# Four sparse attention layers on one core: the first layer's late part in pairs of blocks, list numbers on ScalarE, constants ahead of the statistics

## The chip, the cores and the metric

The kernel runs on one core of a Trainium2 chip. The metric is the device time of one execution in microseconds. Before the change it is 2178.64 us, the median of three runs (2177.56 to 2183.43). The core's engines, as they are called here: PE multiplies matrices, DVE (VectorE) does elementwise work, maxima and sums along the free axis, ACT (ScalarE) does functions, copies and casts, POOL (GpSimd) here issues the gathers and scatters through memory, and SP issues the plain transfers. Each engine works through its own instructions in order and waits on semaphores of the others.

## The reference, cut to what matters

Four graph layers run over the same 4096 nodes of 256 features; each adds to `x` what it computes from the normed `x` and the adjacency. About 277 blocks-of-128 neighbour slots cover all edges, since the adjacency is sparse (a node has itself and a handful of others).

```python
h = jnp.maximum(_layernorm(x, axis=-1), 0.0)
x = x + _L0_gnn_ref(h, adj, L0_gnn_W, L0_gnn_a)      # 4 heads
...
def _L0_gnn_ref(h, adj, W, a):
    Wh = (h @ W).reshape(n, heads, d)
    e = s_i[:, None, :] + s_j[None, :, :]
    e = jax.nn.leaky_relu(e, negative_slope=0.2)
    e = jnp.where((adj == 0)[:, :, None], -jnp.inf, e)
    alpha = jax.nn.softmax(e, axis=1)
    out = jnp.einsum('ijh,jhd->ihd', alpha, Wh).reshape(n, heads * d)
    return jax.nn.elu(out)
```

Layers 1 to 3 are of the same kind, with other scores and weights.

## The kernel before, in words

**Scan** (`lists`, `scan`). The adjacency, 64 MB of int32, is read row block by row block (32 blocks of 128 nodes). ACT casts it to 8 bits (`cast`), PE turns each 512 columns into position codes in PSUM, with the constants `mark`, `places` and `stands` (`marks`), DVE takes the eight greatest of every 256 columns (L485) and `merge` (L493, L495) the best 24 of a row. `number(r)` (L502, L505) turns these codes into node numbers, clamped to 0..n; it is two POOL instructions. The order on ACT, PE and DVE is written out by hand as a list of steps: `plan(engine, at, ...)` puts a piece of work at step `at`, four steps to half a row block, eight to a block, 256 in all for the scan's own work, and `run` issues it. POOL's instructions are ordered by the program's scheduler, except that gathers keep their written order (`in_turn`).

**First layer, early part** (`table`, `early`). While the scan goes on, the first layer's table (normed rows times `W`, with the score sums) is made and written to memory, and for each pair of blocks POOL gathers the first six neighbours (`EARLY`, 12 gathers a pair), which DVE, ACT and PE weigh and add up.

**Placing** (`sort`, `to_place`). Nodes are sorted by their number of neighbours. POOL scatters each row block to its sorted place, one scatter to a block: from step 236 on the first 12, the rest after the scan. Two spans of four steps (240 to 243 and 256 to 259) are left free of scatters. When all have landed, `reload` (L693, L707) reads the lists and rows back, in the order `FIRST`.

**First layer, late part** (`layer(0)`). After the sort a block `b` needs `CAPS[b]` slots, so `CAPS[b] - 6` late ones: 17, 8, 7, 6, 6, 5, 5, 4, 4, 4, five times 3, four times 2, four times 1, and none for blocks 23 to 31; 93 in all. POOL issues one gather to a slot (L757), up to four blocks ahead (`AHEAD`), into a ring of slots. A block then passes through

- `scores`: score sums, leaky relu, maximum, difference (DVE L916, L925, L927, L947, L948), exponential (ACT L955);
- `weigh`: sum, reciprocal, shares (DVE L992 to L998), the block's own part (L1023), shares times gathered rows (L1037), and the sum over slots on PE (L1028, L1047);
- `settle`: elu (ACT L1061, L1062, DVE L1072, L1073), norm (DVE L571, L572, L578, L581 to L587, ACT L577, L579), relu (ACT L734), transposes (PE L742), copy (ACT L744);
- `advance`: product with layer 1's weights (PE L750), then the sum into `x` (DVE L1089), two small copies (ACT L1090, L1091), and one scatter of the row into layer 1's table (POOL, L767).

The stages of several blocks are interleaved by hand; the scatter of a block stands in POOL's queue between the gathers of later blocks. Blocks without a late slot (K = 0) pass with L981, L983 in place of scores and weigh.

**Layers 1 to 3** do the same with all 277 slots each. Layer 1's first gather waits until the last row of its table has landed.

Of the kernel before, what the change touches and what calls it, by code (L numbers as in the profile page):

```python
# [19 lines left out]
P = 128  # L20
# [32 lines left out]
FIRST = [31, 30, 29, 28, 0] + [b for k in range(1, 14) for b in (28 - k, k)] + [14]  # L53
# [18 lines left out]
class Sparse:  # L72
# [30 lines left out]
    def constants(self):  # L103
        nc, const = self.nc, self.const
        self.ident = const.tile([P, P], F32, name="s_ident")
        make_identity(nc, self.ident)
        self.ident_bf = const.tile([P, P], BF16, name="s_ident_bf")
        nc.vector.tensor_copy(self.ident_bf, self.ident)
        self.mark = const.tile([P, P], BF16, name="s_mark")
        nc.vector.tensor_scalar(self.mark, self.ident, MARK, None, ALU.mult)  # L110

        self.below = const.tile([P, P], BF16, name="s_below")
        ones = self.ones = const.tile([P, P], BF16, name="s_ones")
        nc.vector.memset(ones, 1.0)
        nc.vector.memset(self.below, -1.0)
        nc.gpsimd.affine_select(
            out=self.below, in_=self.below, pattern=[[-1, P]], compare_op=ALU.is_ge, fill=0.0,
            base=0, channel_multiplier=1,
        )
        self.eps = const.tile([P, 1], F32, name="s_eps")  # L120
        nc.vector.memset(self.eps, EPS)

# [116 lines left out]
    def scan(self, w0, a0):  # L239
# [32 lines left out]
        nc.vector.memset(self.eps, EPS)  # L272
        xl = lambda g: self.keep[:, 4 * g : 4 * (g + 1), 0:D]
# [22 lines left out]
        for k in range(4):  # L296
            stats(0, k)
        next(norms[0])
        scaled(0)
        *_, (self.we0, _) = first  # L300
        cast(2)
        self.constants()
        for g in range(1, 3):
            for k in range(4):
                stats(g, k)
            next(norms[g])
            scaled(g)
            cast(2 * g + 2)
        later = self.weights()
# [47 lines left out]
        for r in range(nt):  # L357
            plan("pool", 8 * (r + 1), lambda r=r: self.number(r))
        whole, last = [], 0
        for j in range(nt // 2):  # L360
            begin = max(4 * (10 + j), 4 * (4 * j + 4))
            stages = self.early(j)
            step = lambda stages=stages: next(stages)
            plan("pool", begin, step)

            last = max(last + 13 if j else begin + 24, begin + 17)
            plan("dve", last, step)
            for k in range(3):
                plan("dve", last + 2 + k, step)
            for k in range(EARLY + 1):  # L370
                plan("pe", last + 6 + 2 * k, step)
            plan("act", last + 2 * EARLY + 8, step)
            whole.append(last + 2 * EARLY + 8)
# [6 lines left out]
        for at in range(end + 1):  # L380
# [30 lines left out]
            if t > halves - 6 and t not in (halves - 4, halves):  # L411
# [85 lines left out]
    def number(self, r):  # L497

        nc, n = self.nc, self.n
        ids = self.pool.tile([P, TOPK - 1], F32, name=f"s_ids_{r}", tag="ids")  # L500
        self.in_turn(
            nc.gpsimd.tensor_scalar(ids, self.top[:, r, 1:], MARK, MARK + n, ALU.max, ALU.min)  # L502
        )
        self.in_turn(
            nc.gpsimd.tensor_scalar(  # L505
                self.ids[:, r, 0 : TOPK - 1], ids, -1.0, MARK + n, ALU.mult, ALU.add
            )
# [57 lines left out]
    def norms_of(self, pool, x, m, name):  # L565

        nc = self.nc
        mv = pool.tile([P, m, 2], F32, name=f"s_mv_{name}", tag="mv", bufs=2)
# [7 lines left out]
        y = pool.tile([P, 3, m], F32, name=f"s_y_{name}", tag="y", bufs=2)  # L576
# [6 lines left out]
        rn = pool.tile([P, 2 * m], F32, name=f"s_rn_{name}", tag="rn", bufs=2)  # L583
# [103 lines left out]
    def reload(self):  # L687

        nc, tc, nt, n = self.nc, self.tc, self.nt, self.n
        by_place = self.placed.rearrange("(b p) k -> p b k", p=P)  # L690
        near = self.near = self.big.tile([P, nt, 32], U32, name="s_near")
        for a, b in ((0, 2), (nt - 2, nt), (2, nt - 2)):
# [13 lines left out]
            for k in {0: [], nt - 2: FIRST[:5], 2: FIRST[5:]}[a]:  # L706
# [70 lines left out]
    def layers(self):  # L777
        tc, nc, nt = self.tc, self.nc, self.nt
        with ExitStack() as ctx:
            big = self.big = ctx.enter_context(tc.tile_pool(name="s_big", bufs=1))  # L780
            self.pool = ctx.enter_context(tc.tile_pool(name="s_main", bufs=2))
# [7 lines left out]
            rx = big.tile([P, nt, D + WL], F32, name="s_rx")  # L789
# [9 lines left out]
            with tc.manual_schedule():  # L799
                self.reload()  # L800
                for l in range(4):
# [3 lines left out]
    def slots(self, l, b):  # L805
        return max(CAPS[b] - EARLY, 0) if l == 0 else CAPS[b]

    def layer(self, l):
# [6 lines left out]
        order = ORDER if l else FIRST  # L815
        todo, held, at = list(order), {}, 0
        made = []

        def fill(i):
            nonlocal at  # L820
            while todo and nt - len(todo) <= i + AHEAD:
# [13 lines left out]
                k0 = EARLY if l == 0 else 0  # L835
                for k in range(K):
                    at_k = self.near[:, j, k0 + k : k0 + k + 1]
# [33 lines left out]
        for i in range(nt):  # L871
            fill(i)
            b, c, d, e = (order[k] if k >= 0 else None for k in (i, i - S, i - N, i - N - 1))
# [13 lines left out]
        z, y, x, w = order[-1:-5:-1]  # L887
# [14 lines left out]
    def scores(self, l, b, mine, g):  # L902


# [3 lines left out]
        if K == 0:  # L908
            return None
        e = pool.tile([P, TOPK, H], F32, name=f"s_e_{l}_{b}", tag="e", bufs=3)  # L910
        ek = e[:, : K + 1, :].rearrange("p k h -> p (k h)")
        if l < 3:
            src = mine[:, D + H : D + 2 * H]
            if l > 0:
                nc.vector.tensor_tensor(e[:, K, :], mine[:, D : D + H], src, ALU.add)
# [8 lines left out]
            el = ek if l > 0 else ek[:, : K * H]  # L924
            nc.vector.scalar_tensor_tensor(el, el, slope, el, ALU.mult, ALU.max)  # L925
            if l == 0:
                nc.vector.tensor_copy(e[:, K, :], mine[:, D : D + H])  # L927
# [45 lines left out]
    def weigh(self, l, b, me, g, p):  # L973
# [5 lines left out]
        if K == 0:  # L979

            nc.vector.reciprocal(tot, self.before[b])  # L981
            mev = pool.tile([P, D], F32, name=f"s_me_{l}_{b}", tag="me", bufs=4)
            nc.vector.tensor_tensor(  # L983
                mev.rearrange("p (h d) -> p h d", h=H), me.rearrange("p (h d) -> p h d", h=H),
                tot.unsqueeze(2).to_broadcast([P, H, D // H]), ALU.mult,
            )
            return mev
        else:
            by_head = p[:, : K + 1, :].rearrange("p k h -> p h k")
            if l == 0:  # L990
                was = pool.tile([P, H], F32, name=f"s_was_{b}", tag="was", bufs=2)
                nc.vector.tensor_tensor(was, p[:, K, :], self.before[b], ALU.mult)  # L992
                nc.vector.tensor_reduce(tot, by_head[:, :, :K], AX.X, ALU.add)
                nc.vector.tensor_tensor(tot, tot, was, ALU.add)
            else:
                nc.vector.tensor_reduce(tot, by_head, AX.X, ALU.add)  # L996
            nc.vector.reciprocal(tot, tot)  # L997
            nc.vector.tensor_tensor(  # L998
                by_head, by_head, tot.unsqueeze(2).to_broadcast([P, H, K + 1]), ALU.mult
            )  # L1000
            mine = p[:, K, :]
# [13 lines left out]
        pairs = l > 1  # L1015
        full = pairs and K % 2 == 0
        if pairs and not full:
            mev = g[:, K, v0 : v0 + D]
        else:
            mev = pool.tile([P, D], F32, name=f"s_me_{l}_{b}", tag="me", bufs=4)  # L1020
        if full:
            nc.vector.tensor_scalar(mine, mine, 0.5, None, ALU.mult)  # L1022
# [4 lines left out]
        if not pairs:  # L1027
            nc.tensor.matmul(acc, lhsT=self.ident, rhs=mev, start=True, stop=(K == 0))  # L1028
        elif full:
# [4 lines left out]
        for k0 in range(0, K, AT_ONCE):  # L1034
# [5 lines left out]
            for k in range(k0, k0 + m, 2 if pairs else 1):  # L1040
                if pairs:
                    nc.tensor.matmul(  # L1042
                        both, lhsT=self.ident, rhs=g[:, k : k + 2, v0 : v0 + D],
                        start=(k == 0 and not full), stop=(k + 2 >= K),
                    )
                else:
                    nc.tensor.matmul(  # L1047
                        acc, lhsT=self.ident, rhs=g[:, k, v0 : v0 + D],
                        start=False, stop=(k + 1 == K),
                    )  # L1050
        return both if pairs else acc

    def settle(self, l, b, acc, made):
# [4 lines left out]
        if l == 0:  # L1058

            ex = pool.tile([P, D], F32, name=f"s_ex_{b}", tag="ex", bufs=2)  # L1060
            nc.scalar.activation(ex, acc, AF.Exp)  # L1061
            nc.scalar.activation(ex, ex, AF.Copy, bias=-1.0)  # L1062
# [8 lines left out]
        if l == 0:  # L1071
            nc.vector.scalar_tensor_tensor(ex, ex, 0.0, xt, ALU.min, ALU.add)  # L1072
            nc.vector.scalar_tensor_tensor(xt, acc, 0.0, ex, ALU.max, ALU.add)  # L1073
        else:
            for part in (acc[:, 0, :], acc[:, 1, :]) if l == 2 else (acc,):
                nc.vector.tensor_tensor(xt, xt, part, ALU.add)
        into = self.rows[b][:, 0:D] if l == 0 else None
        yield from self.normed(pool, xt, f"{l + 1}_{b}", into=into)

    def advance(self, l, b, ht, made):  # L1080
# [5 lines left out]
        if l == 1:  # L1086
            ps = self.times(ht, self.we1, W, name)
            yield
            nc.vector.tensor_tensor(xt, xt, ps[:, 0:D], ALU.add)  # L1089
            nc.scalar.copy(mine[:, D:W], ps[:, D:W])  # L1090
            nc.scalar.copy(self.listed[b][:, W:], self.near[:, b, 0:TOPK])  # L1091
            made.append((self.tab[1], self.own(b), self.listed[b]))
        elif l == 2:
# [591 lines left out]
```

## Time and profile before

| what | value |
|---|---|
| median of three runs | 2178.64 us |
| the profiled execution | 1824.07 us |
| its span, first to last instruction | 1822.3 us |
| POOL, indirect transfers | 924 late gathers and those of layers 1 to 3 (953 ns each), 192 early gathers (946 ns), 96 scatters |
| DVE busy | 1379.5 us, 76% |
| POOL busy | 1185.3 us, 65% |
| PE busy | 991.5 us, 54% |
| ACT busy | 424.5 us, 23% |

The profiled execution is 354.6 us shorter than the median of the runs. Nothing in the profile says where this difference lies; all durations below are from the profiled execution.

The stages, read from the first and last starts of the lines: scan with early part from 0 to 417 us, placing until 429.7, late part of the first layer from 431.7 (first late gather) to 644.3 (first gather of layer 1), then layers 1 to 3.

To read it: a row of the timeline gives start, duration, engine, line, operation, what it writes and reads with its shape, and in brackets the idle time of the engine before it and what ended it. A row of the waits gives the engine and line that waited, what for, the time in total, how often, and the longest. A row of the windows gives, for a stretch, each engine's busy time and number of instructions.

### The profile page before, as it was taken

The page shows a single profiled execution, that of the slowest core. Times are in us where ns is not written, and L with a number is a line of the kernel's source. Part 1 is how long each engine was busy: PE and PEld are TensorE (multiplying, and loading weights), DVE is VectorE, ACT ScalarE, POOL GpSimd, SP SyncE. Part 2 cuts the span into 40 slices and gives each one's busy share as a digit, 9 for nine tenths or more (in the row PEclk, how much of TensorE's full clock was granted, in tenths as well). Part 3 has the DMA queues.
Part 4 walks back from the last instruction along what each step waited for, and adds up shares of the span by engine and source line. Part 5 has one row for each costly group of instructions (what it writes and reads, how often), then busy time and mean ns, then how long its engine had stood idle before and what let it go on. Part 6 is the DMA issues. An engine that isn't in the chain of part 4 may idle for free. (4 is left out here: it accounts for less than half of the span.)

```text
span 1822.3 us, 14325 instructions
## 1 busy us (share of the span) xinstructions
PE 991.5 (54%) x2551; PEld 476.5 (26%) x2551; DVE 1379.5 (76%) x3900; ACT 424.5 (23%) x1240; POOL 1185.3 (65%) x1324
## 2 busy tenths in 40 slices
PE   4877777752676602222323067888684344565455
PEld 3523333220454401111111023434342111221122
DVE  6889989952689718888888167887885587887777
ACT  5864434101244401111111012222222000000000
POOL 1067756676666267777775577777772577776774
PEclk9989889875788855555555578899897676777777
DMA  9899877347633144444444344444443576666763
GB/s 327 280 394 350 288 272 254 101 141 238 190 97 95 45 104 125 131 130 132 131 131 111 76 118 132 130 137 131 137 128 109 159 217 208 208 208 182 210 205 108
DMA packets 123018, 312.89 MB, mean 172 GB/s; under 512 B 31237, under 2 KB 49672, under 8 KB 122921
## 3 DMA queue, kind: packets, MB, share of 16 engines
q0 software_dynamic: 68064, 207.46, 40.2%
q1 hardware_dynamic: 54856, 104.44, 16.3%
q14 instruction: 74, 0.60, 0.1%
q8 instruction: 24, 0.39, 0.1%
HBM read 276.80 MB, written 35.00 MB: 171 GB/s over the span
## 5 line engine op out<-in xcount | busy, mean ns | idle before, releaser
L757 POOL DMA_INDIRECT s_ring<-s_tab,s_near x924 | 883.9, 957 | 352.8 <-issue 192.0
L1042 PE MATMUL s_acc<-s_ring,s_ident 128*128 128x512 f32 x588 | 319.6, 698 | 184.9 <-issue 96.2
L1042 PEld LDWEIGHTS s_acc<-s_ring,s_ident 128*128 128x128 f32 x588 | 130.6, 228 | 369.6 <-issue 244.8
L757 POOL DMA_INDIRECT s_g<-s_tab,s_keep x192 | 183.2, 954 | 65.0 <-issue 56.5
L485 DVE MAX8 s_cand<-s_pt 128x8 f32<-128x256 f32 x512 | 181.6, 414 | 17.5 <-PE s_pt L483 17.0
L1037 DVE TENSOR_TENSOR s_ring<-s_ring,s_shares 128x2048 f32<-128x2048 f32 (+7 forms) x121 | 187.4, 1572 | 0.0
L742 PE MATMUL s_pht<-s_ident,s_h 128*128 128x128 f32 x128 | 34.3, 361 | 247.9 <-ACT s_h L734 247.9
L750 PE MATMUL s_ps<-s_we_l,s_ht 128*128 128x264 f32 x256 | 115.6, 596 | 92.5 <-ACT s_ht L744 92.5
L1008 DVE SCALAR_TENSOR_TENSOR s_acc<-s_ring,s_p,s_acc 128x256 f32<-128x256 f32 x277 | 135.7, 490 | 9.7
L263 ACT ACTIVATE s_low<-s_raw 128x1024 fp8e4<-128x1024 int32 x128 | 134.2, 1049 | 20.6 <-DMA s_raw<-in_adj_dram 17.3
L558 PE MATMUL s_ae<-s_g,s_ident 128*128 128x512 f32 x192 | 116.1, 701 | 37.3 <-DVE s_g L549 37.3
L478 PE MATMUL s_pt<-s_low,s_mark 128*128 128x512 fp8e4 x256 | 108.1, 422 | 33.8 <-DVE s_cand L485 13.3
L916 DVE TENSOR_TENSOR s_e<-s_ring,s_rx 128x8 f32<-128x8 f32 (+12 forms) x87 | 15.7, 181 | 140.1 <-DMA s_ring<-s_tab,s_near 135.3
L935 DVE TENSOR_TENSOR s_ring<-s_ring,s_shares 128x2048 f32<-128x2048 f32 (+7 forms) x48 | 81.1, 1690 | 48.1 <-DMA s_ring<-s_tab,s_near 32.4
L750 PE MATMUL s_ps_kv<-s_wkv,s_ht 128*128 128x512 f32 x128 | 79.2, 750 | 69.9 <-ACT s_ht L744 69.9
L483 PE MATMUL s_pt<-s_places,s_stands 128*128 128x512 bf16 x256 | 106.6, 416 | 1.4 <-DVE s_stands L455 1.4
L955 ACT ACTIVATE s_shares<-s_e 128x32 f32<-128x32 f32 (+8 forms) x87 | 17.5, 201 | 353.3 <-DVE s_e L948 353.3
L577 ACT ACTIVATE s_y<-s_mv,s_eps 128x1 f32<-128x1 f32 x96 | 28.3, 294 | 294.6 <-DVE s_mv L572 294.6
L750 PEld LDWEIGHTS s_ps<-s_we_l,s_ht 128*128 128x128 f32 x256 | 64.3, 277 | 123.9 <-ACT s_ht L744 113.7
L742 PEld LDWEIGHTS s_pht<-s_ident,s_h 128*128 128x128 f32 x128 | 18.3, 172 | 287.8 <-ACT s_h L734 271.8
L938 DVE TENSOR_REDUCE s_e<-s_ring 128x32 f32<-128x2048 f32 (+7 forms) x48 | 81.2, 1692 | 1.7
L502 POOL TENSOR_SCALAR s_ids<-s_top 128x23 f32<-128x23 f32 x32 | 10.1, 314 | 108.7 <-DVE s_top L493 108.4
(195 smaller groups left out, 1692.2 us busy)
## 6 DMA issues: line engine op xcount, KB each, us to landing
s_raw<-in_adj_dram SPq DMA_DIRECT2D x128, 512.0 KB, 8.1
s_ring<-s_tab,s_near POOLq DMA_INDIRECT x924, 3.0
s_rx<-s_placed SPq DMA_DIRECT2D x32, 262.0 KB, 6.8
s_tab<-s_kv SPq DMA_DIRECT2D x32, 256.0 KB, 2.6
s_tab<-s_keep SPq DMA_DIRECT2D x8, 528.0 KB, 6.9
s_tab<-s_rx SPq DMA_DIRECT2D x32, 132.0 KB, 2.0
s_keep<-in_x_dram SPq DMA_DIRECT2D x8, 512.0 KB, 4.1
s_vself<-s_tab SPq DMA_DIRECT2D x32, 128.0 KB, 2.6
```

Source lines behind the costliest of these rows:

```text
L263: nc.scalar.activation(low[r][:, ts(h, n // 4)], raw.pop(q), AF.Copy, saturate=False, accum_out=self.sums[:, r, h : h + 1],)
L478: nc.tensor.matmul(pt, lhsT=self.mark, rhs=lo[:, ts(g, IB)], start=True, stop=False)
L483: nc.tensor.matmul(pt, lhsT=self.stands[:, g, :], rhs=self.places, start=False, stop=True)
L485: nc.vector.max(out=cand[:, g * (IB // CH) + k, :], in_=pt[:, ts(k, CH)])
L558: nc.tensor.matmul(acc, lhsT=self.ident, rhs=g[:, :, k, 0:D], start=False, stop=(k == E - 1))
L750: self.nc.tensor.matmul(ps[:, :width], lhsT=ht[:, c, :], rhs=w[:, c, :], start=(c == 0), stop=(c == KC - 1),)
L757: return self.nc.gpsimd.indirect_dma_start(out=out, out_offset=None, in_=table[:, :], in_offset=bass.IndirectOffsetOnAxis(ap=idx, axis=0),)
L935: nc.vector.tensor_tensor(kq, kq, q.unsqueeze(1).to_broadcast([P, m, D]), ALU.mult)
L938: nc.vector.tensor_reduce(e[:, k0 : k0 + m, :], kq.rearrange("p k (h d) -> p k h d", h=4), AX.X, ALU.add)
L1008: nc.vector.scalar_tensor_tensor(acc, g[:, k, 0:D], p[:, k, :], acc, ALU.mult, ALU.add)
L1037: nc.vector.tensor_tensor(v, v, p[:, k0 : k0 + m, :].unsqueeze(3).to_broadcast([P, m, H, D // H]), ALU.mult)
L1042: nc.tensor.matmul(both, lhsT=self.ident, rhs=g[:, k : k + 2, v0 : v0 + D], start=(k == 0 and not full), stop=(k + 2 >= K),)
```

## The change

Three things change.

**The late part** becomes a function of its own, `late`, that runs over entries of one or two blocks. Two blocks share an entry only if they have the same number of late slots. An entry of two runs `scores`, the shares, the own part, the elu and the second half of the norm as one instruction over both blocks; the products of shares and rows, the statistics, the relu, the transposes, the product with the weights and the sum into `x` stay one to a block. PE sums slot `k` of both blocks in one matmul of 512 columns. Gathers are issued two entries ahead, and the stages of an entry follow each other within three entries. The order of the blocks changes with it.

**The list numbers** (`number`) move from POOL to ACT, as two relus, two steps later; the early gathers of pair `j` come three steps later; the scatters of placing skip only steps 256 to 259.

**Constants first.** `constants()` is called ahead of the first group's statistics; the first group's weight sums come after its `cast`.

Names of small tiles get the group's size, and the branches for the first layer leave `layer`, `scores`, `weigh`, `settle` and `advance`.

```diff
-FIRST = [31, 30, 29, 28, 0] + [b for k in range(1, 14) for b in (28 - k, k)] + [14]
+LATE = [
+    (30, 31), (28, 29), (0,), (26, 27), (1,), (24, 25), (2,), (3, 4), (23,), (5, 6), (7, 8),
+    (9,), (10, 11), (12, 13), (14,), (15, 16), (17, 18), (19, 20), (21, 22),
+]
...
-        for k in range(4):
-            stats(0, k)
-        next(norms[0])
-        scaled(0)
-        *_, (self.we0, _) = first
-        cast(2)
         self.constants()
-        for g in range(1, 3):
+        for g in range(3):
             for k in range(4):
                 stats(g, k)
             next(norms[g])
             scaled(g)
             cast(2 * g + 2)
+            if g == 0:
+                *_, (self.we0, _) = first
...
-            plan("pool", 8 * (r + 1), lambda r=r: self.number(r))
+            plan("act", 8 * (r + 1) + 2, lambda r=r: self.number(r))
...
-            begin = max(4 * (10 + j), 4 * (4 * j + 4))
+            begin = max(4 * (10 + j), 16 * (j + 1) + 3)
...
-            if t > halves - 6 and t not in (halves - 4, halves):
+            if t > halves - 6 and not nt // 2 * 16 <= at < nt // 2 * 16 + 4:
...
-        self.in_turn(
-            nc.gpsimd.tensor_scalar(ids, self.top[:, r, 1:], MARK, MARK + n, ALU.max, ALU.min)
-        )
-        self.in_turn(
-            nc.gpsimd.tensor_scalar(
-                self.ids[:, r, 0 : TOPK - 1], ids, -1.0, MARK + n, ALU.mult, ALU.add
-            )
+        nc.scalar.activation(a, self.top[:, r, 1:], AF.Relu, bias=self.over)
+        nc.scalar.activation(
+            self.ids[:, r, 0 : TOPK - 1], a, AF.Relu, bias=self.none, scale=-1.0
         )
...
+    def late(self):
...
+        def fill(i):
+            while todo and todo[0] <= i + 2:
...
+        def scores(i):
...
+            nc.vector.tensor_tensor(
+                near, gathered(i)[:, :, :, D : D + H],
+                src.unsqueeze(2).to_broadcast([P, m, K, H]), ALU.add,
+            )
+            nc.vector.scalar_tensor_tensor(near, near, 0.2, near, ALU.mult, ALU.max)
+            nc.vector.tensor_copy(e[:, :, K, :], most)
...
+        def weigh(i):
...
+            for u in range(m):
+                for k0 in range(0, K, AT_ONCE):
...
+            for k in range(K):
+                nc.tensor.matmul(
+                    acc, lhsT=self.ident, rhs=g[:, :, k, 0:D], start=False, stop=(k + 1 == K)
+                )
...
+        def settle(i):
+            nc.scalar.activation(ex, acc, AF.Exp)
+            nc.scalar.activation(ex, ex, AF.Copy, bias=-1.0)
+            yield
+            nc.vector.scalar_tensor_tensor(ex, ex, 0.0, xt, ALU.min, ALU.add)
+            nc.vector.scalar_tensor_tensor(xt, acc, 0.0, ex, ALU.max, ALU.add)
...
+            yield
...
+            ps = [self.times(ht[:, u], self.we1, W, f"1_{i}_{u}") for u in range(m)]
+            yield
+            first = LATE[i][0]
+            for u in range(m):
+                nc.vector.tensor_tensor(xt[:, u, :], xt[:, u, :], ps[u][:, 0:D], ALU.add)
...
+            for b in LATE[i]:
+                self.send(self.tab[1], self.own(b), self.listed[b])
+            yield
...
+        for i in range(len(LATE) + 3):
+            fill(i)
+            go_on(i - 2)
+            if i < len(LATE):
+                scores(i)
+            go_on(i - 1)
+            go_on(i - 3)
+            go_on(i - 2)
+            if i < len(LATE):
+                weigh(i)
+                del held[i]
+            go_on(i - 1)
```

`go_on(i)` runs entry `i`'s `settle` to its next `yield`: the first stage is the exponential on ACT, the second elu and statistics, the third relu and transposes, the fourth the copy and the product, the fifth the sum into `x` and the scatters.

## The prediction

> **What bounds the kernel now.** The chain of waits on the page covers only 1% of the span, so it can't be followed back. I read the windows by stage first, to see which engine is full where; then the waits of DVE and POOL in the stages that change; then the timeline at the seams.
>
> ```profile
> core 0: us, PE busy (x) PEld busy (x) DVE busy (x) ACT busy (x) POOL busy (x), PEclk, DMA share, GB/s
> 60.00:80.00 20.00, 19.31 (x97) 13.81 (x96) 17.38 (x65) 19.12 (x45) 0.52 (x2) 1.00 0.91 284
> ...
> 340.00:385.00 45.00, 33.57 (x90) 12.04 (x87) 42.53 (x111) 1.47 (x4) 30.61 (x36) 0.80 0.39 128
> 385.00:431.00 46.00, 17.57 (x27) 6.54 (x26) 9.68 (x21) 1.32 (x3) 32.31 (x37) 0.65 0.46 165
> ```
>
> The scan is DVE's (42.5 of 45 us), but for a stretch from 60 us in which ACT and PE are full. From 385 to 431 DVE is nearly idle: POOL's queue of gathers and scatters sets the end of the placing.
>
> ```profile
> 383.79 0.96 POOL L647 DMA_INDIRECT s_placed<-s_keep,s_pos  x1 [0.30 <-issue]
> 384.78 0.34 POOL L502 TENSOR_SCALAR s_ids<-s_top 128x23 f32<-128x23 f32 x1
> ...
> 386.50 1.08 POOL L757 DMA_INDIRECT s_g<-s_tab,s_keep  x1 [0.49 <-issue]
> ```
>
> The last list is sorted on DVE at 381.06 (end of L493), yet its gathers start at 386.50: POOL is still at six scatters, then at four number instructions. The 12 gathers and 20 scatters behind run without a gap to 427.3.
>
> In the late part (431.7 to 644.3) DVE is busy 146.6 of the 181 us from 463.5 on, and some 15 more are the 0.03 us between its instructions. POOL has 93 gathers at 1.257 us (0.953 and a gap of 0.30) and 32 scatters at about 1.29: 158 us. So both are near the bound; POOL's wait list tells who leads:
>
> ```profile
> POOL s_tab L767 <- ACT s_rx L1091: 36.7, 14, 5.6
> ```
>
> The scatters wait, mostly at the end, for blocks that come out of DVE's chain. One block with K=4 on DVE:
>
> ```profile
> 548.71 0.17 DVE L916 TENSOR_TENSOR s_e<-s_ring,s_rx 128x16 f32<-128x16 f32 x1
> ...
> 549.53 0.41 DVE L1089 TENSOR_TENSOR s_rx<-s_rx,s_ps 128x256 f32<-128x256 f32 x1
> 549.86 0.44 DVE L1072 SCALAR_TENSOR_TENSOR s_ex<-s_ex,s_rx 128x256 f32<-128x256 f32 x1
> ...
> 551.55 0.15 DVE L992 TENSOR_TENSOR s_was<-s_shares,s_rx 128x4 f32<-128x4 f32 x1
> 551.62 0.16 DVE L993 TENSOR_REDUCE s_t<-s_shares 128x4 f32<-128x16 f32 x1
> 551.82 0.16 DVE L994 TENSOR_TENSOR s_t<-s_t,s_was 128x4 f32<-128x4 f32 x1
> 552.01 0.18 DVE L997 RECIPROCAL s_t<-s_t 128x4 f32<-128x4 f32 x1
> ...
> 553.91 0.15 DVE L581 TENSOR_TENSOR s_y<-s_y 128x1 f32<-128x1 f32 x1
> ...
> 554.57 0.16 DVE L916 TENSOR_TENSOR s_e<-s_ring,s_rx 128x4 f32<-128x4 f32 x1
> ```
>
> From start to start that is 5.86 us, and only 1.13 of it is the gathered rows (L1037, 0.27 a slot): a block costs about 4.75 us however few slots it has.
>
> **The late part on DVE.** The 5.86 us divide by starts into scores 0.82, L1089 0.33, elu 0.94, statistics 0.68, L578 0.07, L992 to L998 0.89, L1023 0.34, L1037 1.13, L581 to L587 0.66. A pair does scores, L578, shares and the norm's end once instead of twice: 2.44, less 0.2 for the wider rows (L916 to L948 go from 0.16 at 128x8 to 0.21 at 128x28). The elu's two instructions and L1023 go from two of 256 columns (0.42) to one of 512; the nearest row is L541, 0.68 at 128x512: 0.45 saved. Statistics back to back are 0.56 instead of 0.68 (from the scan's 4.87 to 5.96): 0.12. Together 2.8 us for each of nine pairs with slots, 25. Pairs without slots save 1.5; two of the four lie behind block 0's gathers, so 3. Sum: 28 us of DVE work.
>
> Here a rule stands against the row. The Trainium skill (Perfetto Trace Analysis, Optimizing Scalar/DVE Operations) prices an instruction's overhead on DVE at about 60 ns on SBUF. A pair drops 18 instructions, so the rule gives an estimate of 1.1 us for a pair, 10 for nine. The trace has both: L992 to L993, which don't need each other, start 0.07 apart; L993 to L994 to L997, each needing the last, 0.20. The dropped instructions are mostly such chains, so I take the rows. The 4-dimensional operands are not unknown: the early part's L526 to L549 are of this form over two blocks (0.21 to 0.27 for the small ones).
>
> **The late part on POOL.** The work is unchanged, 158 us, but its order is not. The head is as before: block 0's 17 gathers share the DMA with the 32 row loads (share 1.03), and DVE gets them at 463.5 (it waits 12.2 us there today). By then POOL has sent entries 0 to 4, 25 gathers, and the next in its queue is entry 0's two scatters. They need L1089 of entry 0, which on DVE now stands behind scores and weigh of block 0 (1.0, wait for the shares 0.7, 1.3, and 4.8 for 17 slots), the elu of entry 1 (2.8) and the norm's end and L1089 (1.4): 475.5, with ACT's copies 476. So POOL idles some 12 us; before, it had 33 gathers out by its first scatter at 474.06. From 476 the last gather is 68 gathers and the 21 scatters ahead of it away: 68 x 1.257 + 21 x 1.29 = 112.6, 588.6. I went through the entries with these prices: from entry 2 to 13 POOL leads (12 gathers and two scatters are 17.7 us for a pair of K=6, DVE needs 10.3), DVE from entry 13, whose gathers land at about 562.5 (3.1 us after issue). In a turn of the loop DVE does scores and weigh of one entry, the elu of the one before, the norm's end of the second before and L1089 of the third; by the pieces above, seven turns from there cost 7.9, 7.1, 7.0, 8.1, 7.2, 7.5 and 4.2 us to the elu of the last entry: 611.5. The last two entries then go through relu (two of 0.5), transposes, copy 0.58, four products of 0.5 and L1089 one after the other, about 9 us, and two scatters with landing 4.8: layer 1 starts at 625. Before: 644.3. **Late part: 19 us less.** PE is not in the way: a pair's slot is one matmul of 0.59 (L558, 128x512) for two of 0.38.
>
> Cover: a pair's shares (ACT L955) have only L1089 on DVE beside them (0.33 or 0.66), where elu and statistics (1.7) hid them; a single entry may show 0.3, six times 2 us at most, and in POOL's stretch nothing.
>
> **Numbers on ACT.** Two ACT instructions for a list: nearest L577, with a pointer bias, 0.30; they replace 0.30 and 0.23 on POOL. At step 8r+10 ACT would wait for the sort of step 8r+7; in 36 to 82 us ACT reaches that step just after the sort (Ln at 40.36, sort done 39.8; 58.50 against 57.9). Its casts are 8 to 28 steps ahead, and its exponentials wait for DVE anyway, so what queues behind it is not hurt. But from 60 to 82 ACT idles only 1.35 of 22 us: two lists add 0.9, so I put **+1 us** (bounds 0 and 3).
>
> **Placing.** With the free span 240 to 243 gone, all 12 early scatters go out from 351.2 on, 15.4 us, ending at 366.6; the 12 gathers of pair 14 (3 steps later, behind them) to 381.6; DVE meets them at 381 and waits 3 us, which nothing needs. The last list is ready at 381.06 + 0.6 on ACT; the last gathers run 382 to 397 instead of 386.5 to 401.5, the 20 scatters to 422.6. **-4.6 us** (bounds -6 and 0, if the scheduler puts scatters between). The three steps of delay cost nothing: POOL starts when the list is there.
>
> **Constants first.** Ten DVE instructions, 2.4 us, move from 12 to 14.4 into the idle time before 4.87, pushing the first statistics by some 0.6. The next statistics wait for `x` at 15.35 and the first relu comes at 24.15 behind `x` of group 2, so the gain is hidden: 0. The transfers keep their order. The two memsets lie there too. Fewer buffers for the own part in layers 2 and 3 (4 to 3), and the new tile pool behind `late`, fall into layer 1's wait of 37.5 us or wait for nothing: 0.
>
> **Sum:** 1824.07 - 19 - 4.6 + 1 = 1801.5, so -22.6. The runs stand 354.6 above the profiled execution, and no view shows where; I carry it as it is: 2178.64 - 22.6 = **2156 us**. If it stretched everything alike (factor 1.194), it would be 2152.
>
> **Rivals.**
> - *DVE's 28 us all arrive* (POOL's head stall is filled): late part -30, 2178.6 - 33.6 = 2145. For it: POOL idled some 22 us before, too. Against: two scatters stand in front of 68 gathers.
> - *POOL takes the late part's gain*: only the placing's remains, 2175. For it: POOL's 158 us against 181.
> - *Slower*: POOL's queue, two entries deep instead of four blocks, stops at every scatter of entries 3 to 13, as the 14 waits on ACT L1091 did, 2.6 us each: 11 x 2.6 = 29, so +6, 2185. It decides above 2 us an entry. For it: each scatter now waits for two L1089 and three ACT copies behind the exponential of the next sum. Against: in my pass DVE is 5 to 10 us ahead there.
> - *The numbers stall ACT* so that casts come late: each of 32 waits would need to cost 0.7 us of DVE time to take the gain; 13.3 us of PE's waits on DVE say DVE leads.
>
> **Chances.** Forecast (2144 to 2167) 0.62; more (below) 0.10; the gain mostly lost 0.14, of which some 0.08 lies within 0.3% (6.5 us, what a measurement can tell); slower by more 0.14. So faster 0.78, same 0.08, slower 0.14. The range takes in the scaled sum and the lost gain and leaves the slower case out: 2134 to 2174.
>
> **What would show it.** Right: the gap between the late part's first gather and layer 1's first falls from 212.6 to some 193; a POOL gap of about 12 us near 464 to 476; DVE's pair at 7 to 8 us; the last early gather some 4.6 us earlier relative to the last sort; 60 to 85 us 1 us longer. Wrong: POOL gaps before scatters in the middle, DVE waits on L955 above 0.5, or waits on L750 in every entry.

## The result, and the profile after

| | changed | before | ratio, 95% interval |
|---|---|---|---|
| median, 12 runs each | 2186.31 us (2174.53 to 2193.06) | 2180.94 us (2176.24 to 2187.58) | 1.0027 (1.0008 to 1.0046) |
| forecast | 2156.0 us (2134 to 2174) | 2178.64 us | 0.990 |

The gain of 22.6 us did not come; the change costs some 5 us, about 0.3%.

**The chips on which this was measured showed two kinds of execution:** the unchanged kernel took 1824.4 to 1825.1 us (medians) on three of them and 2149.6 and 2171.1 us on two, and no execution lay between. The profile of before that the prediction was read from (1824.07 us) is like the first kind, the runs beside it and the result above like the second. Below they are "the 1825 kind" and "the 2150 kind", and a ratio is always between kernels on one chip. Stages are read from one profiled execution of each run.

The page of the changed kernel was taken on the 2150 kind (span 2187.5 us). Its windows, in the columns of before (length, then busy time and instructions of PE, PEld, DVE, ACT, POOL; granted clock, DMA share, GB/s), for the stretch with ACT and PE full, for the whole late part and for layer 1:

```profile
60.00:80.00 20.00, 19.89 (x96) 15.05 (x97) 16.99 (x63) 19.70 (x47) 0.00 (x0) 0.91 0.92 278
...
490.00:719.00 229.00, 116.13 (x352) 73.35 (x352) 129.17 (x422) 62.31 (x192) 122.13 (x125) 0.74 0.40 115
719.00:1223.00 504.00, 90.12 (x192) 46.86 (x192) 286.80 (x984) 53.45 (x192) 262.64 (x277) 0.50 0.33 90
```

And the late part and layer 1 of the first profile of before, in the same view:

```profile
431.00:644.00 213.00, 126.58 (x424) 90.70 (x424) 153.90 (x620) 78.34 (x279) 122.08 (x125) 0.76 0.43 124
644.00:1015.00 371.00, 90.13 (x192) 46.83 (x192) 287.52 (x984) 53.40 (x192) 264.13 (x278) 0.50 0.46 122
```

Layer 1 has the same instructions in both, and the same busy times to 1.5 us on every engine, yet it takes 504 us instead of 371. The granted clock is 0.50 in both. So the 133 us are idle time, not slower work. In the late part the edit did to DVE what it was meant to: 198 instructions fewer and 24.7 us less busy. But the stretch is 229 us instead of 213. (The clock of 0.91 in the first row doesn't belong to the kind: the same kernel has 1.00 there in e4, on the 2150 kind, and 0.91 in e9, on the 1825 kind.)

What POOL waits for in that stretch (total us, times, longest):

```profile
POOL s_tab L772 <- ACT s_rx L959: 34.5, 6, 16.0
POOL s_ring L762 <- issue: 24.1, 78, 0.6
POOL s_tab L772 <- DMA s_tab<-s_rx,s_near: 19.5, 11, 1.8
POOL s_tab L772 <- issue: 12.9, 12, 2.6
```

The third line is a scatter (L772) that waits for another scatter's landing. The profile of before has that once in its late part, for 1.1 us:

```profile
POOL s_tab L767 <- DMA s_tab<-s_rx,s_near: 1.1, 1, 1.1
```

### The profile page after: what moved, and what is told of

Read it like the earlier page. It is cut to its first block, busy times and chain, and to the rows that moved or that the text cites. A ratio compares the mean times of both kernels' runs of the same rounds, so it can differ in the third digit from the quotient of the medians.

```text
span 2187.5 us, 13885 instructions
## 1 busy us (share of the span) xinstructions
PE 1001.9 (46%) x2462; PEld 464.9 (21%) x2479; DVE 1359.4 (62%) x3704; ACT 425.2 (19%) x1217; POOL 1163.0 (53%) x1260
## 4 chain that ended last, share of the span: by engine, by line
DVE 23%; issue 10%; another core or an unknown queue 7%; PE 7%; POOL 5%; DMA 2%; ACT 1%; DVEq 0%; POOLq 0%; SPq 0%; ACTq 0%
POOL s_ring L762 5%; DVE s_acc L1160 4%; PE s_acc L1189 4%; DVE s_ring L1185 3%; DVE s_ring L1103 2%; PE s_ps_kv L755 2%; DVE s_e L1106 2%; DMA s_ring<-s_tab,s_near 1%; DVE s_rx L1209 1%; DVE s_st L575 1%; PE s_ps_q L755 1%; DVE s_kv L1228 1%; DVE s_m L1115 1%; DVE s_y L586 1%
## 5 line engine op out<-in xcount | busy, mean ns | idle before, releaser
L1185 DVE TENSOR_TENSOR s_ring<-s_ring,s_shares 128x2048 f32<-128x2048 f32 (+7 forms) x96 | 159.1, 1685 | 0.0
L1103 DVE TENSOR_TENSOR s_ring<-s_ring,s_shares 128x2048 f32<-128x2048 f32 (+7 forms) x48 | 81.1, 1690 | 51.1 <-DMA s_ring<-s_tab,s_near 32.1
L755 PEld LDWEIGHTS s_ps<-s_we_l,s_ht 128*128 128x128 f32 x256 | 68.9, 292 | 185.7 <-ACT s_ht L749 77.6
L491 PE MATMUL s_pt<-s_places,s_stands 128*128 128x512 bf16 x239 | 102.0, 427 | 0.0
L581 ACT ACTIVATE s_y<-s_mv,s_eps 128x1 f32<-128x1 f32 (+1 forms) x83 | 24.5, 295 | 387.7 <-DVE s_mv L576 306.2
L1178 PE MATMUL s_acc<-s_me,s_ident 128*128 128x512 f32 x60 | 42.1, 791 | 100.9 <-issue 35.4
L1123 ACT ACTIVATE s_shares<-s_e 128x40 f32<-128x40 f32 (+7 forms) x64 | 13.2, 206 | 323.3 <-DVE s_e L1116 143.0
L772 POOL DMA_INDIRECT s_tab<-s_rx,s_near x32 | 31.7, 990 | 74.9 <-ACT s_rx L959 34.5
```

The source lines that it names most:

```text
L491: nc.tensor.matmul(pt, lhsT=self.stands[:, g, :], rhs=self.places, start=False, stop=True)
L755: self.nc.tensor.matmul(ps[:, :width], lhsT=ht[:, c, :], rhs=w[:, c, :], start=(c == 0), stop=(c == KC - 1),)
L1103: nc.vector.tensor_tensor(kq, kq, q.unsqueeze(1).to_broadcast([P, m, D]), ALU.mult)
L1185: nc.vector.tensor_tensor(v, v, p[:, k0 : k0 + m, :].unsqueeze(3).to_broadcast([P, m, H, D // H]), ALU.mult)
```

## The experiments

Theory A at the outset: the profile of before is not typical, and the idle time swallows what the edits save. Theory B: POOL's shallower queue stops at its scatters. Theory C: the late part gains as forecast and the scan loses it. Theory D came after the first four runs: in a pair, the second scatter waits for the first one to land.

**The two kernels again (e1, e4), and each half of the change alone (e2, e3).** All on one chip of the 2150 kind. e2 takes `late`, `LATE` and what goes with them and leaves the scan as before; e3 the reverse.

```
e2:  plan("pool", 8 * (r + 1), lambda r=r: self.number(r))      as before; late() of the change
e3:  plan("act", 8 * (r + 1) + 2, lambda r=r: self.number(r))   and constants() first; layer(0) as before
```

> The kernel before, unchanged, profiled once more. Theory A: the execution of 1824 us, from which every duration of the prediction came, is not what this kernel usually does; this profile comes out near 2180 us, with idle time on DVE, PE and ACT that no wait explains from about 100 us on, as in the profile of the changed kernel, and with layers 1 to 3 at about 1460 us (1467 in the changed kernel) instead of 1178. Rival B: the profile of before is typical and the change alone brings the idle time; this one comes out near 1824 us again.

> The late part in pairs, with the numbers on POOL, the old steps of gathers and scatters, and the constants behind the first statistics as before. Theory A (both parts are swallowed by idle time of all engines): within 0.3% of before. Theory B (POOL's queue of two entries stops at the scatters): slower than before by 5 to 15 us, the late part itself longer than in before. Theory C (the late part gains as predicted, the scan loses it): faster by some 15 to 20 us.

> The scan of the change (numbers on ACT, early gathers three steps later, free span moved, constants first) with the late part of before. Theory A: within 0.3% of before. Theory B: faster by up to 5 us. Theory C (ACT's wait for the sort holds the casts or the exponentials up): slower by 20 to 25 us.

> The changed kernel, unchanged, profiled on the same chip as the three others, for its stages. Theory A: layers 1 to 3 take within 1% of what they take in before's second profile, late part and scan differ by a few us each. Theory B: late part longer than before's by 10 us or more. Theory C: late part shorter by 15 us or more, the time to the first late gather longer by 20 or more.

Measured: e1 2153.56 us and e4 2148.79 us (one execution each), e2 ratio 1.0002 (0.9976 to 1.0028), e3 ratio 1.0051 (1.0021 to 1.0081). C falls: the late part gains nothing there (228.6 us in e2, 221.9 in e1), and the scan's part alone loses. e1, the kernel before, is itself at 2153 us, so the change did not bring the idle time. The timeline of DVE in e1, merging one list, shows how it looks:

```profile
115.22 0.28 DVE L495 MATCH_REPLACE8 s_cand<-s_top,s_cand 128x128 f32<-128x128 f32 x1
116.82 0.29 DVE L493 MAX8 s_top<-s_cand 128x8 f32<-128x128 f32 x1 [1.32 <-DVE s_cand L495]
118.22 0.09 DVE L495 MATCH_VALUE_LOAD s_cand<-s_top,s_cand 128x8 f32 x1 [1.11 <-DVE s_top L493]
```

DVE waits here for DVE: an instruction that needs the one before it starts 1.1 to 1.3 us after that one's end, where 0.03 is usual in the first profile.

Counted over whole profiles, for instructions of DVE that wait for DVE alone: on the 1825 kind none of some 2,100 starts more than 0.2 us after the end of the one before it. In the seven profiles of the 2150 kind 846 of 14,830 start more than 0.6 us after it, up to 6.5 us. None of these 846 lies in the stretches in which POOL issues no gather or scatter (the time before the first gather at 96 us and every pause of over 20 us, counted from 5 us after the last issue, above all the ends of layers 1 and 2; 2,582 instructions). Such a stretch in e1, the end of layer 1, with 200 instructions of DVE and 2 of POOL:

```profile
1128.00:1200.00 72.00, 19.71 (x42) 10.23 (x42) 56.92 (x200) 11.47 (x40) 1.08 (x2) 0.50 0.06 19
```

Plain transfers alone do not do it: from 40 to 60 us e1 moves 310 GB/s, and nothing is late. So on that kind DVE's own signals are late only while POOL's indirect transfers go on. Why they are late on these chips and not on the others, no run shows.

**The scatters free of one another (e5, e6).** The rows of a block go to different places, so the scatters need no order among themselves. The small memset on POOL separates neighbours in the queue.

```
 for b in LATE[i]:
+    nc.gpsimd.memset(self.between, 0.0)
     sent = self.send(self.tab[1], self.own(b), self.listed[b])
+    self.tc.declare_no_dep(sent.ins, group="rows", reason="places differ")
...
+    layer 1's first gather depends on all 32 scatters
```

> Late part in pairs, scan as before, and the scatters of the late part no longer wait for one another's landing (they write different rows; layer 1's first gather waits for all of them). Theory D (the pair's second scatter, directly behind the first on POOL, waits some 2 us for the first to land, which two scatters of single blocks never met): POOL's waits of s_tab on DMA s_tab, 21.4 us (11 times) in the late part of pairs alone, go; the late part falls from 228.6 us to 200 to 210, so below the 221.9 of single blocks, and the time is 12 to 22 us below the kernel before (ratio about 0.992). Theory A (the idle time between dependent instructions of these executions swallows the gain, whatever the scatters wait for): late part at least 223, ratio 0.998 to 1.002.

> The kernel before with the same freedom for its late scatters. Theory D: no wait on a landed scatter stands in its list of POOL's waits, since 5 us of DVE or some gathers lie between two scatters of single blocks, so the late part stays at 222 (within 3) and the time is the same. Rival: if the scatters' order costs single blocks too, the late part falls by 10 or more.

These fell on the 1825 kind: e5 1815.06 against 1825.1, ratio 0.9941 (0.9928 to 0.9953), late part 200.0 us; e6 1.0001 (0.999 to 1.0012), late part 212.7 (before: 212.6). Single blocks lose nothing by the order: their scatters start 3.2 us or more apart.

**The change and the pairs alone on the 1825 kind (e9, e11), and the change with free scatters (e10).**

> The changed kernel once more, since the runs fall on chips of two kinds: on some the kernel before takes 1825 us, on others 2150 to 2180, with idle time between dependent instructions. Theory D (in the late part a pair's second scatter waits for the first to land): the late part is 11 to 20 us longer than that of the pairs without that wait (200.0 on a chip of the 1825 kind), so 211 to 220, which takes the whole gain of the pairs; the placing keeps its 5 us. On the 1825 kind: 1818 to 1825, ratio 0.996 to 1.000; on the other kind as measured before, ratio 1.000 to 1.004. Theory A (only the idle time of the slower kind swallows the pairs' gain): on the 1825 kind the late part is 200 to 203, ratio 0.989 to 0.992.

> The pairs alone, scan as before. Theory D: late part 211 to 220 on the 1825 kind of chip (200.0 without the wait, 212.6 in single blocks), ratio 1.000 to 1.004; on the slower kind as measured before, late part 228, ratio 1.000. Theory A: on the 1825 kind 200 to 203, ratio 0.994.

> The changed kernel with the late part's scatters free of one another's landing. Theory D: 11 to 20 us below the changed kernel on either kind of chip; on the 1825 kind ratio to before 0.988 to 0.992, on the slower kind 0.993 to 0.997. Theory A: within 3 us of the changed kernel.

e9: 1815.95 against 1824.41, ratio 0.9953 (0.9939 to 0.9966), late part 214.2. e11: 1828.78, ratio 1.0024 (1.0014 to 1.0034), late part 215.2. e10: 1803.39, ratio 0.9882 (0.9867 to 0.9897), late part 200.1. So with the landing wait the pairs alone lose 4.4 us; without it they gain 10 (e5). The whole change gains 8.5 with the wait (e9) and 21 without it (e10). POOL in e9, at a pair's two scatters:

```profile
484.64 0.94 POOL L762 DMA_INDIRECT s_ring<-s_tab,s_near  x1 [0.30 <-issue]
485.88 1.00 POOL L772 DMA_INDIRECT s_tab<-s_rx,s_near  x1 [0.30 <-issue]
488.77 0.98 POOL L772 DMA_INDIRECT s_tab<-s_rx,s_near  x1 [1.88 <-DMA s_tab<-s_rx,s_near]
490.06 0.99 POOL L762 DMA_INDIRECT s_ring<-s_tab,s_near  x1 [0.30 <-issue]
```

and in e10:

```profile
487.56 1.00 POOL L773 DMA_INDIRECT s_tab<-s_rx,s_near  x1 [0.19 <-issue]
488.56 0.11 POOL L963 MEMSET s_between<- 128x1 f32 x1
488.87 0.99 POOL L773 DMA_INDIRECT s_tab<-s_rx,s_near  x1 [0.19 <-issue]
490.16 0.99 POOL L763 DMA_INDIRECT s_ring<-s_tab,s_near  x1 [0.30 <-issue]
```

From one scatter to the next it is 2.89 us with the wait and 1.31 without. The later gathers stand behind it in the queue, and the DVE work behind the gathers. The Trainium skill (DMA: Bandwidth & Descriptors, Anatomy of one DMA — SWDGE (gpsimd) path) puts the fixed part of such a transfer at about 2 us, most of it until the last byte is confirmed landed; here the first scatter landed 2.6 us after its start, the transfer's own time included, which agrees.

**The gathers further ahead (e14), and e10's kernel once more (e13).** In e14 `fill` reaches four entries ahead:

```
-    while todo and todo[0] <= i + 2:
+    while todo and todo[0] <= i + 4:
```

> The same with the gathers four entries ahead of the sums instead of two. If POOL's stall of 15 us at the head (it waits there for the first entry's sums with nothing else to send) sets the late part's length, filling it brings 7 to 12 us more: late part 188 to 193 on the 1825 kind, 1791 to 1797. If DVE's chain sets it, or the scatters now wait behind more gathers, at most 3 us, or a loss.

> The changed kernel with free scatters again. On the 1825 kind of chip: 1803, ratio 0.988, as measured. On the slower kind, theory D: the landing wait is as long there (16 to 21 us of POOL's waits in the late part), so 10 to 20 us go, late part 208 to 218 for 228, ratio to before 0.993 to 0.999 with the scan's loss in it. Rival (the idle time of the slower kind hides the landing wait): late part 225 or more, ratio 1.001 to 1.004.

e14: 1796.04 against 1825.06, ratio 0.9845 (0.9824 to 0.9866), late part 191.1 us. POOL now has 44 gathers out before its first scatter, not 25, and its longest wait for ACT there is 6.4 us, not 15; that is worth 7.4 us in the medians (e13: 1803.43). This is the fastest version on the 1825 kind; on the other it was not run. e13: ratio 0.9879 (0.9862 to 0.9897), late part 200.6.

**The scan in parts (e7, e8, e12, e15, e16, e18).** e7, e12, e15 and e18 are one kernel: the numbers on ACT, and with them the three steps of delay and the placing's span, but the constants in their old place. e8 has only the constants first; e16 only the placing's span:

```
-    if t > halves - 6 and t not in (halves - 4, halves):
+    if t > halves - 6 and t != halves:
```

> The kernel before with only the numbers on ACT (and the three steps later that the early gathers are planned, and the placing span that goes with it); DVE's constants where they were. If the numbers and the new order of POOL's queue cause the loss of the scan (0.5% with both parts), it is all here: ratio 1.003 to 1.006, the last sort 10 to 14 us later than the 434.3 of the kernel before. If the constants cause it: ratio 1.000.

> The kernel before with only DVE's constants first. By the prediction and by the profile of the changed kernel they are hidden: within 1 us of the kernel before to the first gather, ratio 1.000 (within 0.002). If the constants were the cause of the scan's loss: ratio 1.003 to 1.006.

> The numbers on ACT alone (with the early gathers' three steps and the placing span), again. On the 1825 kind: ratio 0.993 to 0.997, as measured. On the slower kind: if the numbers cause the scan's loss there, ratio 1.003 to 1.006 and the last sort 10 to 14 us later; if not, 1.000 or below.

> The kernel before with only the free span of the early placing (steps 240 to 243) given up, numbers on POOL. If the placing is what gains on the 1825 kind (forecast -4.6): late part's first gather 4 to 6 us earlier, ratio 0.997. If the numbers' leaving POOL is what gains: within 2 us of before, ratio 1.000.

> The numbers on ACT alone. On the 1825 kind: ratio 0.993 to 0.996. On the slower kind: 1.003 to 1.006 if they are the scan's loss there, 1.000 or below if not.

On the 1825 kind: numbers on ACT 0.9933 (0.9916 to 0.9949), 0.9947 and 0.9949 (e15) on three chips, a gain that neither reading of e7 had foreseen; constants 0.9991 (0.9985 to 0.9998); the span alone 1.0000 (0.999 to 1.0011). On the 2150 kind (e18): 2181.18 against 2171.05, ratio 1.0040 (1.0022 to 1.0059). So the constants are nothing much, the span by itself is nothing, and the numbers on ACT, with span and delay, are worth some 9 us on one kind and cost some 10 on the other. The numbers without the span were not run.

**Free scatters on the 2150 kind (e17).**

> Pairs with free scatters, scan as before. On the 1825 kind of chip: ratio 0.994, as measured. On the slower kind, where the pairs with the landing wait were 1.0002 (late part 228.6): theory D: late part 208 to 218, ratio 0.991 to 0.996. Rival (the idle time there hides the landing wait): 225 or more, ratio 0.998 to 1.002.

2171.53 against 2171.05: ratio 0.9997 (0.9976 to 1.0019). The rival holds there: even without the landing wait the pairs bring nothing. The late part in e17:

```profile
489.00:713.00 224.00, 112.56 (x352) 70.62 (x352) 129.27 (x422) 62.71 (x192) 127.02 (x158) 0.77 0.41 118
```

and in e1, with single blocks on the same kind:

```profile
482.00:704.00 222.00, 127.07 (x424) 91.20 (x424) 153.64 (x620) 79.07 (x279) 122.25 (x125) 0.76 0.41 119
```

Here e17 has 223.8 us from first gather to first gather, and e1 221.9. DVE is busy 24 us less and idle 26 us more. One stop of e17 in the timeline, where a K = 6 pair waits for its sums (line numbers a few above the changed kernel's; L922 is the sum over slots, L933 and L934 the exponential and its minus one, L936 the elu):

```profile
586.02 5.31 PE L922 MATMUL s_acc<-s_ring,s_ident 128*128 128x512 f32 x12
...
591.17 0.38 PE L953 MATMUL s_pht<-s_ident,s_rx 128*128 128x128 f32 x2
...
597.73 0.60 ACT L933 ACTIVATE s_ex<-s_acc 128x512 f32<-128x512 f32 x1 [9.09 <-remote]
598.36 0.63 ACT L934 ACTIVATE s_ex<-s_ex 128x512 f32<-128x512 f32 x1
...
599.02 0.69 DVE L936 SCALAR_TENSOR_TENSOR s_ex<-s_ex,s_rx 128x512 f32<-128x512 f32 x1 [9.81 <-ACT s_ex L934]
```

PE is through the sums by 591.3 (its ends are modelled, but its next instruction starts at 591.17), ACT starts on them at 597.73: 6.4 us later. Of PE's semaphore, the only one that ACT waits for, the trace has a rise at 597.71 and the one before it at 592.07. So ACT starts at once when the rise comes, and it is the rise that is late. POOL goes on gathering meanwhile, so nothing is short of rows.

## Why the prediction was wrong, step by step

**The time carried over.** "The runs stand 354.6 above the profiled execution, and no view shows where; I carry it as it is." This is the step that failed for the result. It takes the difference for a constant that both kernels pay alike. It is idle time, and the changed kernel pays more of it. Of the 329.5 us between the first profile and e1, 51 lie ahead of the late part, 9 in it and 269 behind it. The late part of single blocks goes from 212.6 to 221.9 us, 9 more; that of pairs with free scatters from 200.0 (e5) to 223.8 (e17), 24 more. So the pairs gave 1.0002 with the landing wait (e2) and 0.9997 without it (e17): DVE's saving (24 us) came back as DVE's idle time (26 us). What is left for the result is the scan's part, which costs 0.4 to 0.5% there (e18, e3). The measured 1.0027 fits that within the intervals.

**The late part, 19 us.** Wrong on the profile's own kind as well: it took 2.6 us more (212.6 to 215.2, e11), not 19 less. The term of the sum that failed is POOL's: 21 scatters at 1.29 us behind the head. In a pair the second scatter follows the first directly and waits for its landing, which makes 2.89 us of 1.3. The number of POOL's instructions is unchanged, as I wrote, but not their cost: single blocks' scatters are far enough apart to hide that order. The code showed it: `to_place` declares its scatters independent, the late part's `send` does not. The wait is worth 14 to 15 us (200.0 to 200.1 without it, 214.2 to 215.2 with it). With it gone, the rest of the working holds closely:

```profile
460.02 0.94 POOL L763 DMA_INDIRECT s_ring<-s_tab,s_near  x1 [1.09 <-DMA s_ring<-s_tab,s_near]
460.97 0.11 POOL L963 MEMSET s_between<- 128x1 f32 x1
476.08 1.00 POOL L773 DMA_INDIRECT s_tab<-s_rx,s_near  x1 [15.00 <-ACT s_rx L961]
```

These lines of e10 are the head: a stall of 15 us (12 forecast), and the first scatter at 476.08 (476 forecast). That the two times agree is luck: e10's late part begins at 427.7, and the sum began it at 431.7. Head and last gather (588.6) are each 4 us later from its start than forecast, and the tail from there to layer 1 is 39.2 instead of 36.4. That is 200 us for 193. (Before its first scatter the kernel before has 32 gathers out, not 33.)

**DVE's 28 us.** Right: busy time fell from 153.9 to 128.9 us (e9), and 198 instructions' spaces of 0.03 add up to 6 at most. The rule that I weighed, some 60 ns for an instruction, would have given 10. Measured are 25 us of busy time for 198 instructions, 0.126 us each, part of it saved in the wide rows. The sentence behind the 60 ns in the Trainium skill (Perfetto Trace Analysis, Optimizing Scalar/DVE Operations) puts an instruction's profiled latency at about twice that; I left it out, and it is nearer. The rows were right to be preferred.

**Placing -4.6, numbers on ACT +1.** The sum of -3.6 came near what the 1825 kind shows at the first late gather, 4.4 us (e7 against e6), 6.0 (e12 against e11) and 9.4 (e15 against e16) earlier, and 9 in the medians. But both terms were wrong, and that their sum is near is luck. The span alone brings nothing (e16). The numbers on ACT do delay the last sort, by 7.8, 6.2 and 2.9 us in the same pairs of runs, more than the 0 to 3 forecast in two of the three. What pays for it is an order that I overlooked. With the numbers on POOL, those of the last list stand in its queue ahead of all 12 gathers of the last pair, the six for the list before included; so all 12 wait for the last sort. With the numbers on ACT those six go out before it. e9 at the last list, where now ACT is the one that waits:

```profile
385.09 0.95 POOL L762 DMA_INDIRECT s_g<-s_tab,s_keep  x1 [0.30 <-issue]
...
386.13 0.31 ACT L509 ACTIVATE s_ids<-s_top,s_over_mark 128x23 f32<-128x23 f32 x1 [11.57 <-DVE s_top L501]
386.48 0.31 ACT L510 ACTIVATE s_keep<-s_ids,s_none_n 128x23 uint32<-128x23 f32 x1
387.06 0.94 POOL L762 DMA_INDIRECT s_g<-s_tab,s_keep  x1 [1.02 <-ACT s_keep L510]
```

The first row is the sixth of the earlier list's gathers. POOL is on the next one 1.0 us after the sort (386.10), where it took 5.4 in the first profile, and six gathers follow instead of 12 (7.5 us less). Together that is the 12 us by which the way from the sort to the first late gather is shorter (50.8 in e6, 38.6 in e7).

On the 2150 kind the way is only 8 to 9 us shorter (48.4 in e1, 39.6 in e3): there POOL starts its 12 gathers 1.2 us after the sort before the change too (435.5 in e1), so the six gathers are all that is saved. The last sort comes 12 to 13 us later with the numbers on ACT (434.3 in e1, 447.5 in e3; 440.3 in e17, 452.4 in e18). That makes the first late gather some 4 us later. The rest of the loss lies behind it, where the instructions are the same: e3's late part takes 232.4 us and e1's 221.9, both of single blocks (e18: 226.4). That the path to the gathers now goes over one engine more, each with its late signals, fits the later sort, but was not tested; what lengthens the late part is open.

**Constants first, 0.** Right to within 2 us (0.9991, 0.9985 to 0.9998).

**The sum** on the profile's own kind was 1801.5: the change measures 1815.95 there, and 1803.39 with its scatters free. The rival that came nearest is the slower one, POOL's queue stopping at its scatters; its place was right and its reason wrong (the first scatter's landing, not L1089), and on the 2150 kind that stop is not what takes the gain (e17).

**Left open:** why signals are late on the 2150 kind while indirect transfers go on, and whether those chips differ or only their condition at the time: each chip was measured at one time alone. Why the numbers on ACT cost more there than the later sort explains. e14's version was not measured there.

## What to carry to other kernels

Before a sum is made against a profile, the profile must be of the kind of execution that the runs are: 16% between the two was a reason to take another profile, not to carry a constant. When an edit brings two transfers of one kind side by side, ask whether the second is ordered behind the first's landing, and look in the code for the places where that order was already lifted. Where engines are idle on signals, work taken off the busiest one can come back as idle time, as DVE's 24 us did on the 2150 kind. Where one queue holds work for two results, ask whether the part that is ready stands behind the part that is not: six gathers did here.

## What was not expected of the hardware

The same program with the same busy times (DVE 1379.5 and 1382.7 us) differs by 325 to 347 us between chips (medians), and in layer 1 all of the 125 us that e1 has more is idle time, at the same granted clock (0.50). On the 2150 kind DVE's signals to itself come up to 6.5 us late while POOL's gathers and scatters go on, and on time when it issues none; one from PE to ACT came 6.4 us late. In layer 1 of e1 69 of DVE's 760 steps that wait for DVE alone begin over 0.6 us after the end of the step before, in the first profile none; the median is 0.035 us on both kinds. There are also fewer records of a rise: e1 has 2227 for the 3269 instructions that raise DVE's semaphore, the first profile 3270 for 3269, and none lacks before the first gather. Whether rises are put together there or records lost, the trace does not tell.
